# The shared expert's up products of one token block: sixteen 512-column matmuls replaced by seven products of two by two blocks

## The chip, the cores and the metric

The kernel runs on one core of one Trainium2 chip. The metric is the device time of one execution in microseconds (us); lower is better. The profile counts from the first to the last instruction (the span); a little time lies around the span and is part of the device time.

Engines, as the profile names them: PE (TensorE, matmuls) with PEld (its weight loads), DVE (VectorE), ACT (ScalarE), POOL (GpSimd, which here issues the gathers and scatters), SP (SyncE, which issues the plain DMAs).

## The reference

The input has 16 sequences of 128 tokens with 512 features, 2048 tokens in all. First comes cross attention with a residual, which the change does not touch. Then a mixture of experts:

```python
g = einsum('td,eid->tei', x, w1); u = einsum('td,eid->tei', x, w3)
a = silu(g) * u
routed = einsum('tei,edi,te->td', a, w2, comb)        # 32 experts, 8 for each token
sh = silu(x @ shared_w1.T) * (x @ shared_w3.T) @ shared_w2.T
out = routed + sh                                     # and the residual
```

Here `x` is the layer-normed input of 512 features, an expert's inner width is 256, and everything is float32. The change is in `sh`: the two "up" products `x @ shared_w1.T` and `x @ shared_w3.T` for the last 512 of the 2048 tokens.

## The kernel before

**Layout.** The normed tokens lie transposed in one buffer, `xall`, as four blocks `xnT[k]` of 512 tokens (128 partitions x 4 feature chunks x 512 tokens). `sup` holds the shared up weights (both matrices), `sdn` the shared down weight. `acts[k]` receives silu(g)*u of block `k`.

**Shared expert.** `shared_up(k, i, ...)` does one half (`i`) of the inner width of block `k`: four accumulating matmuls of 128x512 into one PSUM bank for `g`, four for `u`, a Silu on ACT (tile `ssl`) and a product on DVE (tile `sa`). `shared_down(b)` does two matmuls of 128x512 for the 128 tokens of sequence `b`, and `add_down` adds the result to the residual `xs[b]` on DVE and starts the DMA that writes it to the output. A product or an addition is not issued at once: it is put into the list `products` and issued some step later.

**Order.** The four compute engines run in an order written out by hand: each engine executes its instructions in the order in which the Python code issues them. The shared expert's matmuls fill PE while other engines work. Six of the eight halves (blocks 0 to 2) are done during the attention's end and the routing (`route`, then the loop over `slot_tokens`). After `finish_tokens` the list of each slot's token is known and POOL starts to gather rows. At this point the two halves of block 3 and eight down products are left. They are issued as follows:

```python
up_matmuls(2 * ND)                       # g and u of block 3, half 0: 8 matmuls
for f in evictions() + evictions(): f()
transpose_to(5)                          # the first five gathered slices
up_matmuls(2 * ND)                       # half 1: 8 matmuls
for f in evictions() + evictions(): f()
...
for i, b in enumerate(downs):            # b = 8..15
    shared_down(b, ps_p)
    ...                                  # transposes, block copies, weight sums, additions
```

**Gathered rows.** `gather(j)` (POOL) fetches the 128 rows of slice `j` into one of six buffers `xgs`; `transpose(j)` turns it on DVE in blocks of 32 (`blocks`) and `weigh(j)` takes its weights (tile `own`), after which the buffer is free for slice `j+6`. `block_copies(k)` copies the turned blocks of expert `k` (k in the order of execution) to `x_of[k % 3]`, which overlays `xall`: for experts 0 and 1 three quarters of these copies are on ACT and one quarter on DVE.

**Experts.** Expert 0 is computed directly (`up`, eight groups of four matmuls 128x256). Experts 1 to 30 use seven products of two by two blocks instead of eight (Strassen's scheme in Winograd's form): `weight_sums(k)` and `token_sums(k)` make four sums each on DVE, `product` issues the matmuls, and `seven(k)` is a generator that does one of the seven products at each `next` and schedules, with `soon`, the ACT copy of the first product (`p1`), the DVE additions (`u2`, `z`) and the Silu and multiplication one or more steps later. The fifth, sixth and seventh product accumulate into the banks of the first, third and fourth, so they need the earlier reader of that bank to be done. The bank pool `ps_p` has six banks, taken in turn; the last eight shared down products use it too.

Of the kernel before, what the change touches and what calls it, by code (L numbers as in the profile page):

```python
# [9 lines left out]
F32 = mybir.dt.float32  # L10
# [3 lines left out]
ALU = mybir.AluOpType  # L14
# [4 lines left out]
P = 128  # L19
# [8 lines left out]
NW = 3  # L28


ROOM = [704, 660, 640, 628, 616, 608, 604, 600, 596, 584, 580, 560, 544, 540, 540, 536]
# [6 lines left out]
ORDER = [18, 0, 11, 1, 29, 2, 3, 4]  # L38
# [8 lines left out]
def tile_xattn_moe(  # L47
# [15 lines left out]
    nc = tc.nc  # L63
    B, S, D = x.shape
    E, _, ND, I = w1.shape
    NI = I // P
    KV = D // HD // G
    NT = B
    NTB = NT // 4
    TB = 512  # L70
# [17 lines left out]
    xnT = [  # L88
        xall[:, k * ND * TB : (k + 1) * ND * TB].rearrange("p (d t) -> p d t", d=ND)
        for k in range(NTB)  # L90
    ]
# [58 lines left out]
    fp = x_only.enter_context(tc.tile_pool(name="fp", bufs=2, side="right"))  # L150
# [10 lines left out]
    sup = const.tile([P, 2, ND, I], F32, name="sup")  # L161
# [82 lines left out]
    def gate_logits(b, ps_lg):  # L244
# [15 lines left out]
    NA = 3  # L260
    aall = sap.tile([P, NA * NI * 2 * HM], F32, name="sa")
    acts = [
        aall[:, k * NI * TB : (k + 1) * NI * TB].rearrange("p (i t) -> p i t", i=NI)
        for k in range(NTB)
    ]
    acts_of = [
        aall[:, r * NI * 2 * HM : (r + 1) * NI * 2 * HM].rearrange("p (i t) -> p i t", i=NI)
        for r in range(NA)
    ]
# [733 lines left out]
    def experts(ups, in_order, later, products):  # L1003
# [8 lines left out]
        wup = [wp.tile([P, 2, ND, I], F32, name=f"wup{r}") for r in range(NW)]  # L1012
# [32 lines left out]
        shared = ExitStack()  # L1045
# [28 lines left out]
        def all_ups():  # L1074
            for k, i in ups:
                banks = iter(
                    [(ps_y, "y"), (ps_z, "y")]
                    if (k, i) == (1, 1)
                    else [(ps_p, "p")] * 2
                    if k == NTB - 1  # L1080
                    else [(ps_gu, "gu")] * 2
                )

                def bank():
                    pool, tag = next(banks)
                    return pool.tile([P, TB], F32, tag=tag, name="gu")

                yield from shared_up(k, i, bank, later, products)
# [3 lines left out]
        def up_matmuls(n):  # L1092
            for _ in range(n):
                next(matmuls, None)
# [259 lines left out]
        downs = iter(range(B))  # L1354
        held = []

        def evictions():
            nonlocal held
            fs = later + held
            held = list(products)  # L1360
            later.clear()
            products.clear()
            return fs
# [18 lines left out]
        pieces = []  # L1382
# [82 lines left out]
        def soon(f, after=1):  # L1465
            jobs.setdefault(now + after, []).append(f)
# [27 lines left out]
        M = TB // 2  # L1494
        sums = {}

        def weight_sums(k):


            a11, a12, a21, a22 = (  # L1500
                wup[k % NW][:, :, d : d + 2, ts(i, P)] for i in range(2) for d in (0, 2)
            )
            s1, s2, s4 = (
                tp.tile([P, 2, 2, P], F32, tag=name, name=name) for name in ("s1", "s2", "s4")
            )
            sums[k] = s1, s2, a21, s4
            return [
                lambda o=o, a=a, b=b, op=op: nc.vector.tensor_tensor(o, a, b, op)
                for o, a, b, op in (
                    (s1, a21, a22, ALU.add),  # L1510
                    (s2, s1, a11, ALU.subtract),
                    (a21, a11, a21, ALU.subtract),
                    (s4, a12, s2, ALU.subtract),
                )
            ]

        def halves_of(k):

            h = ROOM[ORDER[k]] // 2
            return [  # L1520
                x_of[k % NX][:, d : d + 2, i * h : (i + 1) * h] for d in (0, 2) for i in range(2)
            ]
# [29 lines left out]
                        skip_group_check=not first,  # L1552
                    )

        def add(out_, a, b):
            soon(lambda: nc.vector.tensor_tensor(out_, a, b, ALU.add))  # L1556

        def seven(k):


            h = ROOM[ORDER[k]] // 2
            act = acts_of[k % NA]
            a11, a12, _, a22 = (
                wup[k % NW][:, :, d : d + 2, ts(i, P)] for i in range(2) for d in (0, 2)
            )
            s1, s2, s3, s4 = sums[k]
            b11, _, b21, b22 = halves_of(k)
            t1, t2, t3, t4 = tsums.pop(k)
            both = 2 * h <= TB
            size = M if both else HM  # L1570

            def new(name, n, size, bufs=2):
                if name == "sg":
                    t = xnp.tile([P, TB], F32, tag="xn2", name=name, bufs=4)
                else:
                    size_of = 4 * M if name == "z" else TB
                    t = late.tile([P, size_of], F32, tag=name, name=name, bufs=bufs)
                return t[:, 0 : n * size].rearrange("p (n t) -> p n t", n=n)[:, :, 0:h]

            def silu(to, of, after):  # L1580
                soon(lambda: nc.scalar.activation(to, of, AF.Silu), after)

            def times(to, a, b, after):
                soon(lambda: nc.vector.tensor_tensor(to, a, b, ALU.mult), after)

            act0, act1 = act[:, 0, 0:h], act[:, 1, 0:h]
            act2 = act[:, :, h : 2 * h]

            for w in (slice(0, 2),) if both else (slice(0, 1), slice(1, 2)):

                many = w.stop - w.start

                def bank():
                    p = ps_p.tile([P, TB], F32, tag="p", name="p")
                    return p[:, 0 : many * size].rearrange("p (n t) -> p n t", n=many)[:, :, 0:h]

                pa, p1 = bank(), new("p1", many, size, 1)
                product(pa, a11[:, w], b11)
                soon(lambda p1=p1, pa=pa: nc.scalar.copy(p1, pa))
                yield  # L1600
                pb, u2 = bank(), new("u2", many, size)
                product(pb, s2[:, w], t2)
                add(u2, p1, pb)
                yield
                pc = bank()
                z = new("z", 2 * many, size)
                z0, z1 = z[:, 0:many], z[:, many : 2 * many]
                product(pc, s1[:, w], t1)
                add(z1, u2, pc)
                yield  # L1610
                pd = bank()
                product(pd, s3[:, w], t3)
                add(z1, z1, pd)
                yield
                product(pa, a12[:, w], b21, first=False)
                if both:
                    sl = new("sg", 1, TB)[:, 0]
                    silu(sl, pa[:, 0], 1)
                    times(act0, sl, pa[:, 1], 2)
                elif w.start == 0:  # L1620
                    silu(act0, pa[:, 0], 1)
                else:
                    times(act0, act0, pa[:, 0], 1)
                yield
                product(pc, s4[:, w], b22, first=False)
                add(z0, u2, pc)
                if both:
                    sl = new("sg", 2, M)
                    silu(sl, z[:, 0::2], 2)
                    times(act2, sl, z[:, 1::2], 3)  # L1630
                elif w.start == 0:
                    silu(act2, z, 2)
                else:
                    times(act2, act2, z, 2)
                yield
                product(pd, a22[:, w], t4, first=False)
                add(u2, u2, pd)
                if both:
                    sl = new("sg", 1, TB)[:, 0]
                    silu(sl, u2[:, 0], 2)  # L1640
                    times(act1, sl, u2[:, 1], 3)
                elif w.start == 0:
                    silu(act1, u2[:, 0], 2)
                else:
                    times(act1, act1, u2[:, 0], 2)
                yield
# [250 lines left out]
        def transpose_to(j):  # L1897
            nonlocal n_turned
            while n_turned < j:
                transpose(n_turned)  # L1900
                n_turned += 1
                gather_next()

        gather_next()
        up_matmuls(2 * ND)
        for f in evictions() + evictions():
            f()
        transpose_to(5)
        up_matmuls(2 * ND)
        for f in evictions() + evictions():  # L1910
            f()
        copies = [*block_copies(0), *block_copies(1, slices=range(4, 7))]
        copies = [f for _, _, f in copies]
        downs = list(downs)
        for i, b in enumerate(downs):
            shared_down(b, ps_p)
            transpose_to(min(6 + i, last_slice(3)))
# [114 lines left out]
        in_order.close()  # L2032
        ctx.close()

    pieces = [(k, i) for k in range(NTB) for i in range(NI)]
    left_over = attention_small()
    experts(pieces[1:], in_order, *left_over)
    left = nc.values_load(
# [64 lines left out]
```

## Time and profile before

| | us |
|---|---|
| median of 4 runs (849.90 to 851.83) | 850.63 |
| profiled execution, device time | 849.99 |
| its span | 848.1 |
| outside the span | 1.9 |
| PE busy | 830.0 (98%) |
| DVE busy | 686.4 (81%) |
| ACT busy | 670.8 (79%) |
| POOL busy | 479.0 (56%) |

The granted TensorE clock is 0.997 of full speed over the span. Where the code issues one float32 matmul, the profile shows two MATMUL rows, so 16 matmuls of block 3 are 32 rows. A row of the timeline gives start, duration, engine and line, operation, the written and the read tiles, shapes and a count; in square brackets stands how long the engine was idle before and what ended that.

### The profile page before, as it was taken

How to read it: one execution, taken by the hardware profiler on the slowest of the kernel's cores; microseconds unless marked ns; L12 is line 12 of the kernel's file. 1: busy time of each engine (PE TensorE's matmuls, PEld its weight loads, DVE VectorE, ACT ScalarE, POOL GpSimd, SP SyncE). 2: the span in 40 equal slices, each digit the busy share in tenths (PEclk: the TensorE clock that was granted, in tenths of full speed). 3: DMA queues.
4: the chain of work that ended last, by engine and by line, in shares of the span. 5: the costliest groups of instructions: out<-in, count | busy, mean ns of one | idle time of the engine just before them, and what ended most of it. 6: DMA issues, size and time to landing. Idle time of an engine off the chain costs nothing.

```text
span 848.1 us, 14951 instructions
## 1 busy us (share of the span) xinstructions
PE 830.0 (98%) x4847; PEld 604.1 (71%) x4847; DVE 686.4 (81%) x1660; ACT 670.8 (79%) x1225; POOL 479.0 (56%) x574
## 2 busy tenths in 40 slices
PE   8999999999999999999999999999999999999995
PEld 6555545546676866777787878787888899887663
DVE  7987888849787977988898989898989999986210
ACT  5989723638988896988988989988898999998631
POOL 4597730053445676465538585765757666654553
PEclk9999999999999999999999999999999999999998
DMA  9211104456666798577769697978788878785653
GB/s 298 81 52 64 58 33 159 152 157 199 177 153 152 172 190 240 135 187 177 190 156 228 166 218 179 219 170 197 180 201 191 209 193 184 195 209 123 97 83 50
DMA packets 59878, 137.22 MB, mean 162 GB/s; under 512 B 12168, under 2 KB 16392, under 8 KB 59792
## 3 DMA queue, kind: packets, MB, share of 16 engines
q0 software_dynamic: 32032, 69.25, 41.9%
q1 hardware_dynamic: 27680, 66.81, 23.5%
q8 instruction: 40, 0.66, 0.3%
q14 instruction: 46, 0.38, 0.1%
q10 hardware_dynamic: 80, 0.13, 0.1%
HBM read 96.71 MB, written 46.73 MB: 169 GB/s over the span
## 4 chain that ended last, share of the span: by engine, by line
PE 85%; DVE 5%; POOL 3%; issue 3%; ACT 2%; DMA 2%; POOLq 0%; ACTq 0%
PE p L1546 43%; PE y L1787 17%; PE gu L285 7%; PE y L1687 5%; PE y L1340 3%; PE m L491 2%; POOL out_dram L1659 2%; PE sc L473 2%; DMA out_dram<-yp,token 2%; PE gu L1476 2%; DVE o L501 1%; PE m L453 1%; ACT xall L1441 1%; DVE st L95 1%; PE tok L989 1%
## 5 line engine op out<-in xcount | busy, mean ns | idle before, releaser
L1441 ACT COPY xall<-blocks 32x512 f32<-32x512 f32 (+4 forms) x684 | 360.4, 527 | 10.9 <-DVE blocks L1444 0.9
L1659 POOL DMA_INDIRECT out_dram<-yp,token x122 | 201.0, 1648 | 153.0 <-ACT yp L1799 42.4
L1403 POOL DMA_INDIRECT xgs<-rows,token x138 | 152.9, 1108 | 120.2 <-DMA out_dram<-x 54.0
L1546 PE MATMUL p<-xall,wup 128*128 128x270 f32 (+27 forms) x720 | 185.9, 393 | 0.0
L1546 PEld LDWEIGHTS p<-xall,wup 128*128 128x128 f32 x720 | 136.7, 190 | 31.6 <-issue 4.7
L1546 PE MATMUL p<-t,s 128*128 128x270 f32 (+27 forms) x480 | 123.6, 394 | 0.0
L1546 PEld LDWEIGHTS p<-t,s 128*128 128x128 f32 x480 | 91.1, 190 | 20.2 <-issue 3.2
L1444 DVE STREAM_TRANSPOSE blocks<-xgs 128x512 f32<-128x512 f32 x138 | 97.0, 703 | 0.0
L1687 PE MATMUL y<-wdn,sa 128*32 128x512 f32 (+2 forms) x288 | 78.7, 596 | 0.0
L1659 POOL DMA_INDIRECT out_dram<-yw,token x28 | 45.0, 1605 | 49.5 <-DMA out_dram<-yw,token 29.8
L483 ACT ACTIVATE p<-sc 128x1024 f32<-128x1024 f32 x64 | 62.1, 1024 | 10.0 <-PE sc L473 9.3
L1556 DVE TENSOR_TENSOR z<-u,p 128x270 f32<-128x270 f32 (+27 forms) x96 | 48.4, 504 | 21.5 <-PE p L1546 21.2
L1546 PE MATMUL p<-t,wup 128*128 128x270 f32 (+27 forms) x240 | 63.8, 396 | 0.0
L1546 PE MATMUL p<-xall,s 128*128 128x270 f32 (+27 forms) x240 | 63.4, 395 | 0.0
L285 PE MATMUL gu<-xall,sup 128*128 128x512 f32 x128 | 58.7, 599 | 0.0
L1799 ACT ACTIVATE yp<-yp,wt 128x256 f32<-128x256 f32 (+1 forms) x96 | 54.3, 608 | 3.6 <-DVE yp L1778 2.6
L1778 DVE TENSOR_TENSOR yp<-sdn,y 128x512 f32<-128x512 f32 x72 | 49.1, 682 | 8.2 <-PE y L1787 4.6
L1546 PEld LDWEIGHTS p<-t,wup 128*128 128x128 f32 x240 | 45.0, 190 | 14.7 <-DVE z L1556 2.8
L1546 PEld LDWEIGHTS p<-xall,s 128*128 128x128 f32 x240 | 45.3, 190 | 13.0 <-issue 3.9
L1787 PE MATMUL y<-sup,sa 128*128 128x256 f32 x192 | 49.9, 382 | 1.5 <-ACT sdn L1842 1.4
L1687 PEld LDWEIGHTS y<-wdn,sa 128*32 128x32 f32 (+2 forms) x288 | 28.0, 145 | 30.1 <-issue 28.2
L1787 PE MATMUL y<-wdn,sa 128*128 128x256 f32 x192 | 49.3, 379 | 0.0
(235 smaller groups left out, 1392.8 us busy)
## 6 DMA issues: line engine op xcount, KB each, us to landing
wup<-in_w_dram SPq DMA_DIRECT2D x64, 512.0 KB, 6.6
wdn<-in_w_dram SPq DMA_DIRECT2D x32, 512.0 KB, 4.8
rows<-xn SPq DMA_DIRECT2D x16, 256.0 KB, 2.2
out_dram<-x SPq DMA_DIRECT2D x16, 256.0 KB, 3.0
x<-in_x_dram SPq DMA_DIRECT2D x15, 256.0 KB, 6.0
xgs<-rows,token POOLq DMA_INDIRECT x138, 5.4
out_dram<-yp,token POOLq DMA_INDIRECT x122, 5.6
cTs<-in_cT_dram SPq DMA_DIRECT2D x4, 256.0 KB, 5.2
```

Of the source, the lines that this page charges most:

```text
L285: nc.tensor.matmul(acc, lhsT=sup[:, w, d, ts(i, P)], rhs=xnT[k][:, d, :], start=(d == 0), stop=(d == ND - 1),)
L483: nc.scalar.activation(p, sc, AF.Exp, scale=1.0 / HD**0.5)
L1403: nc.gpsimd.indirect_dma_start(out=t, out_offset=None, in_=rows[:, :], in_offset=bass.IndirectOffsetOnAxis(ap=token[:, j : j + 1], axis=0) ...
L1441: yield on_ACT, 1 + many, lambda dst=dst, of=of, copy=copy: copy(dst, of)
L1444: nc.vector.transpose(blocks[:, j % NB_BUF, :], xgs[:, j % NG_BUF, 0:D])
L1546: nc.tensor.matmul(acc[:, i, 0:h], lhsT=w[:, i, d, :], rhs=x[:, d, :], start=(first and i == d == 0), stop=(i == outs[-1] and d == 1), ski ...
L1556: soon(lambda: nc.vector.tensor_tensor(out_, a, b, ALU.add))
L1659: ins = nc.gpsimd.indirect_dma_start(out=flat, out_offset=bass.IndirectOffsetOnAxis(ap=token2[:, k - 1 : k] if a else token[0:b, j : j + 1 ...
L1687: nc.tensor.matmul(y[c0:c1, :], lhsT=acts_of[k % NA][:, i, col : col + c1 - c0], rhs=wdn[k % NW][:, i, :], start=(i == 0), stop=(i == NI - 1),
L1778: then(lambda: nc.vector.tensor_tensor(to, a, b, op), after)
L1787: nc.tensor.matmul(acc[:, r, :], lhsT=a[:, ts(r, P)], rhs=b, start=(first and r == 0), stop=(r == 1), skip_group_check=not first,)
L1799: lambda r=r, at=at: nc.scalar.activation(to[:, r], of[:, r], AF.Copy, scale=wt[:, at : at + 1]),
```

## The change

The two halves of block 3 are no longer done by `shared_up`. Instead `seven` gets a form for the shared expert: block 3 of the tokens is cut into two by two blocks (256 features x 256 tokens each), the up weight `sup` likewise, and seven products of four matmuls 128x256 replace sixteen matmuls of 128x512. The sums are made on DVE right before (`shared_sums`): S1, S2, S3, S4 of the weights (S3 in place in `sup`) and t1, t2, t3, t4 of the tokens (t3 in place in `xnT[3]`; t1, t2 and t4 in the unused `xnT[1]`). Temporaries (`p1`, `u2`, `z`) lie in the unused `xnT[2]`. Two down products, b = 8 and 9, stand behind the second and the fifth of the seven; six are left for the loop behind. The five transposes that stood together between the halves are spread behind the third to seventh product.

```diff
-        up_matmuls(2 * ND)
-        for f in evictions() + evictions():
+        later_jobs = {}
+        turn = 0
+        ...
+        k = NTB - 1
+        sums_of_k = shared_sums(k)
+        of_shared = seven(k, True, lambda f, after=1: later_jobs.setdefault(turn + after, []).append(f))
+        downs = list(downs)
+        for f in sums_of_k[:4]:
             f()
-        transpose_to(5)
-        up_matmuls(2 * ND)
-        for f in evictions() + evictions():
+        for down_too in (0, 1, 0, 0, 1, 0, 0, 0):
+            behind = list(products)
+            products.clear()
+            next(of_shared, None)
+            if down_too:
+                shared_down(downs.pop(0), ps_p)
+            for f in behind:
+                f()
+            run_later()
+            for f in sums_of_k[4:] if turn == 1 else ():
+                f()
+            transpose_to(max(0, min(turn - 2, 5)))
+        while later_jobs:
+            run_later()
+        for f in products:
             f()
+        products.clear()
         copies = [*block_copies(0), *block_copies(1, slices=range(4, 7))]
         copies = [f for _, _, f in copies]
-        downs = list(downs)
         for i, b in enumerate(downs):
             shared_down(b, ps_p)
```

```diff
+        def shared_sums(k):
+            b11, b12, b21, b22 = shared_halves(k)
+            t1, t2, t4 = (
+                xnT[1].rearrange("p d (a t) -> p (d a) t", t=M)[:, 2 * i : 2 * i + 2]
+                for i in range(3)
+            )
+            tsums[E + k] = t1, t2, b12, t4
+            s1, s2, s3, s4 = weight_sums(E + k, sup)
+            t1, t2, t3, t4 = (
+                lambda o=o, a=a, b=b: nc.vector.tensor_tensor(o, a, b, ALU.subtract)
+                for o, a, b in ((t1, b12, b11), (t2, b22, t1), (b12, b22, b12), (t4, b21, t2))
+            )
+            return [s1, s2, t1, t2, t3, s3, s4, t4]
...
+        def seven(k, shared=False, soon=soon):
...
-    pieces = [(k, i) for k in range(NTB) for i in range(NI)]
+    pieces = [(k, i) for k in range(NTB - 1) for i in range(NI)]
```

As built, the order on each engine from the end of the routing to expert 0 is (matmuls as the code counts them, transposes T with their weighing):

| | before | after |
|---|---|---|
| PE | 16 of 128x512, downs 8 to 15 | P1 (4 of 128x256), P2, down 8, P3, P4, P5, down 9, P6, P7, downs 10 to 15 |
| DVE | add of down 7, product, T0 to T4, product, T5 | add of down 7, S1, S2, t1, t2, t3, S3, S4, t4, u2, add of down 8, z, T0, z, T1, T2, add of down 9, product, z, T3, u2, T4, two products, T5 |
| ACT | Silu, Silu, then the copies of expert 0 | copy of p1, three Silus, then the copies of expert 0 |

In the loop over the downs the copies are dealt over six turns instead of eight. The orders of POOL and SP are unchanged, and so is everything from expert 0 on.

More of the change, by code (lines that the diff above doesn't have):

```diff
@@ L1078, in all_ups @@
                     if (k, i) == (1, 1)
-                    else [(ps_p, "p")] * 2
-                    if k == NTB - 1
                     else [(ps_gu, "gu")] * 2
@@ L1495, in experts, with weight_sums @@
         sums = {}
-        def weight_sums(k):
+        def weight_sums(k, of=None):
+            of = wup[k % NW] if of is None else of
             a11, a12, a21, a22 = (
-                wup[k % NW][:, :, d : d + 2, ts(i, P)] for i in range(2) for d in (0, 2)
+                of[:, :, d : d + 2, ts(i, P)] for i in range(2) for d in (0, 2)
             )
@@ L1553, in product, with shared_halves, add @@
                     )
[L1555 to L1562, printed above, removed]
+        def shared_halves(k):
+            return [xnT[k][:, d : d + 2, i * M : (i + 1) * M] for d in (0, 2) for i in range(2)]
+        def shared_sums(k):
[12 more added lines that the diff above has]
+        def seven(k, shared=False, soon=soon):
+            h = M if shared else ROOM[ORDER[k]] // 2
+            act = acts[k] if shared else acts_of[k % NA]
             a11, a12, _, a22 = (
-                wup[k % NW][:, :, d : d + 2, ts(i, P)] for i in range(2) for d in (0, 2)
-            )
-            s1, s2, s3, s4 = sums[k]
-            b11, _, b21, b22 = halves_of(k)
-            t1, t2, t3, t4 = tsums.pop(k)
+                (sup if shared else wup[k % NW])[:, :, d : d + 2, ts(i, P)]
+                for i in range(2)
+                for d in (0, 2)
+            )
+            s1, s2, s3, s4 = sums[E + k if shared else k]
+            b11, _, b21, b22 = shared_halves(k) if shared else halves_of(k)
+            t1, t2, t3, t4 = tsums.pop(E + k if shared else k)
             both = 2 * h <= TB
             size = M if both else HM
+            def add(out_, a, b):
+                soon(lambda: nc.vector.tensor_tensor(out_, a, b, ALU.add))
             def new(name, n, size, bufs=2):
+                if shared:
+                    if name == "sg":
+                        t = fp.tile([P, TB], F32, tag="ssl", name="ssl")
+                        return t.rearrange("p (n t) -> p n t", n=n)[:, :, 0:h]
+                    at = dict(p1=0, u2=2, z=4)[name]
+                    return xnT[2].rearrange("p d (a t) -> p (d a) t", t=M)[:, at : at + n]
                 if name == "sg":
@@ L1904, in experts, with run_later @@
         gather_next()
-        up_matmuls(2 * ND)
-        for f in evictions() + evictions():
-            f()
-        transpose_to(5)
-        up_matmuls(2 * ND)
-        for f in evictions() + evictions():
+        later_jobs = {}
+        turn = 0
+        def run_later():
+            nonlocal turn
+            turn += 1
+            for f in later_jobs.pop(turn, []):
+                f()
[4 more added lines that the diff above has]
+        for f in sums_of_k[:4]:
+            f()
+        for down_too in (0, 1, 0, 0, 1, 0, 0, 0):
[8 more added lines that the diff above has]
+            for f in sums_of_k[4:] if turn == 1 else ():
+                f()
+            transpose_to(max(0, min(turn - 2, 5)))
+        while later_jobs:
+            run_later()
+        for f in products:
             f()
+        products.clear()
         copies = [*block_copies(0), *block_copies(1, slices=range(4, 7))]
         copies = [f for _, _, f in copies]
-        downs = list(downs)
         for i, b in enumerate(downs):
```

## The prediction

> **What bounds the kernel now.** I read the page first, then the chain of waits around the change, then the timelines of PE, DVE, ACT and POOL from 172 to 240 us.
>
> ```profile
> PE 830.0 (98%) x4847; PEld 604.1 (71%) x4847; DVE 686.4 (81%) x1660; ACT 670.8 (79%) x1225; POOL 479.0 (56%) x574
> ```
>
> PE is busy nearly throughout. The chain of waits (start, duration, what, rows) passes through nothing but PE at the change:
>
> ```profile
> 172.68 1.76 PE y L1340 x4
> 174.44 13.73 PE gu L285 x32
> 188.18 13.73 PE y L1340 x32
> 201.91 13.81 PE gu L1476 x64
> 215.72 4.73 PE p L1546 x16
> 220.46 1.72 PE y L1687 x4
> 222.18 8.28 PE p L1546 x28
> ```
>
> So here PE's own time, and any new wait of PE, goes one to one into the end. (The chain books a matmul 0.16 us later than the timeline starts it; below I use the timeline.) Now the two engines that feed PE, DVE first:
>
> ```profile
> 174.48 0.69 DVE L1350 TENSOR_TENSOR x<-y,x 128x512 f32<-128x512 f32 x1 [0.53 <-PE y L1340]
> 181.42 0.69 DVE L296 TENSOR_TENSOR sa<-ssl,gu 128x512 f32<-128x512 f32 x1 [6.25 <-PE gu L285]
> ...
> 189.99 0.67 DVE L1508 TENSOR_TENSOR s<-wup 128x512 f32<-128x512 f32 x1
> 190.70 0.69 DVE L1508 TENSOR_TENSOR s<-s,wup 128x512 f32<-128x512 f32 x1
> 191.31 0.68 DVE L1508 TENSOR_TENSOR wup<-wup 128x512 f32<-128x512 f32 x1
> 191.91 0.68 DVE L1508 TENSOR_TENSOR s<-wup,s 128x512 f32<-128x512 f32 x1
> ...
> 206.40 0.71 DVE L1444 STREAM_TRANSPOSE blocks<-xgs 128x512 f32<-128x512 f32 x1
> ...
> 218.20 0.52 DVE L1556 TENSOR_TENSOR u<-p,p 128x352 f32<-128x352 f32 x1 [0.33 <-PE p L1546]
> ```
>
> DVE waits 6.25 us for PE while block 3's first half runs; from 188.3 to 218 it has no gap. The L1508 rows are the sums of an expert, of the size the new ones have: a sum starts 0.61 us after the one before, 0.71 us if it reads its result. ACT:
>
> ```profile
> 185.41 7.53 ACT L1441 COPY xall<-blocks 32x512 f32<-32x512 f32 x12
> 193.85 7.80 ACT L1441 COPY xall<-blocks 32x384 f32<-32x384 f32 x15 [0.92 <-DVE blocks L1444]
> 203.68 0.39 ACT L1485 ACTIVATE sg<-gu 128x256 f32<-128x256 f32 x1 [2.03 <-PE gu L1476]
> ```
>
> Expert 0's copies end at 192.9, 8.8 us before PE starts expert 0 at 201.75. That slack is what the change will use.
>
> **Part 1, PE work.** Removed: 32 rows of 128x512, 13.73/32 = 0.429 us each. Added: 7 x 4 x 2 = 56 rows of 128x256; the nearest row, L1476, has 64 of this shape in 13.81, 0.216 each, so 12.08 (1.73 a product). Saved: 1.65 us. The eight downs cost the same (1.72 each).
> A rule speaks against this. The Trainium skill, "TensorE: Matmul & The Clock Gate", section "Back-to-back issue gap", says that in a stream of weight loads and matmuls the spacing is set by both, about 81 ns at 128 columns and 131 ns at 512. Interpolated to 256 columns (my estimate, 98 ns), 56 rows would cost 1.3 times what 32 wide ones do, and the seven products would lose. The float32 rows here contradict it: 0.216 against 0.429 is proportional to the columns, with the 0.19 us weight load hidden under either.
>
> **Part 2, the wait of the second product.** P1 needs no sum; P2 needs S2 and t2. DVE runs in order, behind the add of down 7, which cannot start before 174.48 as PE finishes that down only then: S1 174.48 + 0.61 = 175.09, S2 + 0.71 = 175.80 (its start), t1 + 0.61 = 176.41, t2 + 0.71 = 177.12, done 177.80, handed over by 177.86. P1 runs 174.28 to 176.01. PE waits 1.85 us, with downs 8 to 15 queued behind P2 on PE. Bounds: 1.7 (the chain's later booking of PE) and 2.0 (a handover of 0.2, as from PE to DVE above). So parts 1 and 2 sum to **+0.2**: the saving is gone at once.
>
> **Part 3, the rest of the seven, hidden.** t3, S3, S4, t4 (177.7 to 180.2) and u2 (180.2) run beside P2 and down 8 (to 181.3). P3 181.3, P4 183.0, P5 184.8, down 9 to 188.2, P6 188.2, P7 189.9 to 191.65. The copy of p1 has ended long before P5; z, 183.2 to 183.9, before P6. Behind P7: u2 191.85 to 192.5, Silu 192.6 to 193.0, last product 193.85 to 194.25. Down 12 is the first to need it, at 195.1; downs 10 and 11 cover it with 0.8 to spare, and without them it would cost 2.6. PE reaches expert 0 at 201.95.
> POOL is moved past nothing, but gathers 1 to 5 now run beside sums. Bounds from rows: 1.00 us for most, 1.54 for the one at 190.00 that began with an L1508 sum. Five times 0.54 makes gather 5 land 2.7 later, still before its transpose at 194.2: nothing. The Trainium skill, "SBUF — State Buffer", section "Who interferes with whom", says that a tensor_tensor with two SBUF inputs blocks GpSimd's reads for the whole instruction; the 1.54 row fits a delay of most of one sum.
>
> **Part 4, the backlog.** In before, T3 ends at 185.0 and T5 at 189.8. After, T3 stands behind z of P6 (190.1) and runs 190.7 to 191.5, T5 194.2 to 195.0. DVE is 5.2 us late, less two adds already made (1.2) and small gaps: the row at 206.40 comes at about 210.0, 3.6 late. ACT starts expert 0's copies at 193.0 behind the last Silu, 7.6 late; it makes up its gaps of 0.92 and 2.03, so the row at 203.68 comes at about 208.3, 4.6 late. Three places where PE meets this:
> - Expert 0 needs 12 copies on ACT (193.0 + 7.53 = 200.5: in time) and four on DVE: T5's end 195.0, four sums and four turns of add, transpose and copy as before (8.3 us from 189.66 to 197.9 in before, one add and one transpose less now) give 202.1. PE waits 0 to 0.5; I take 0.2.
> - Expert 1, first half. PE needs z from DVE for P6 and P7. In before (start of the z adds 219.31 and 221.12, 0.52 each; PE at 223.19 and 224.38) the slack is 3.3 and 2.7 us. DVE arrives at u2 (218.20 in before) 3.6 to 4.5 late (the 0.33 gap is made up, and u2 also waits for ACT's copy of p1, 4.1 to 4.8 late); PE itself is 0.4 late. The wait is between 0.4 and 1.8; I take 1.1.
> - Expert 1, second half. Expert 2's token sums stand before u2 on DVE and wait for ACT's copies, still 3.5 late; slack at P7 there is 2.1, PE then 1.6 late. 0 to 0.8; I take 0.4.
>
> Behind this the gaps of DVE (1.8, 0.5) and ACT (0.8, 0.8, 1.3) between 236 and 245 take up the rest.
>
> **Sum.** +0.2 + 0.2 + 1.1 + 0.4 = +1.9: the profiled execution goes from 849.99 to 851.9 (span 848.1 + 1.9 and 1.9 around it). The median of the runs lies 0.6 above that execution, so I predict 850.63 + 1.9 = **852.5**.
>
> **Rivals.**
> - *Backlog absorbed* (no change): DVE and ACT arrive only as late as their slack. For it: each margin is within 1 us of the lateness. Against it: DVE has no gap from 188 to 218. Parts 1 and 2 and half of the copies' wait remain, +0.2 to +0.6: 850.8 to 851.2.
> - *Sums in time* (faster): S2 and t2 are ready at P1's end. It decides from t2 done by 176.0, and then -1.65: 849.0; each 0.1 later takes 0.1 back. Against it: 3.3 us of chain behind an add that PE itself releases at 174.48. It would need the scheduler to let PE's next down go first, and the order as built has P2 first.
> - *Backlog lasts* (slower still): ACT, 4 us late, does not recover before 245, since its load from 215 to 230 is 14.0 of 15 us. Then the copies for experts 2 and 3 hold DVE's sums, and PE waits 0.5 to 1 us in each of two to four further halves: +3.5 to +5.5, 854.1 to 856.1.
> - That the change does not do what it says is excluded: the built order shows the seven products and two downs between.
>
> **How the numbers follow.** Forecast 0.50 (+1.2 to +2.8), absorbed 0.22, lasting 0.18, faster 0.10. The range takes the first two and most of the third: 850.4 (0.6 under the absorbed case's middle) to 855.0. 0.2% is 1.7 us, about what a measurement of this kernel tells from no change. Of the forecast's band 0.30 lies above it, 0.20 below; so slower 0.30 + 0.18 = 0.48, same 0.20 + 0.22 = 0.42, faster 0.10.
>
> **What would show it.** Right: a PE gap of 1.7 to 2.0 us before the second product, released by DVE; PE at expert 0 within 0.5 of 201.95; ACT's copies of expert 0 from about 193; PE gaps before the sixth and seventh product of expert 1, released by DVE z. Wrong: P2 starting near 176.0, or no PE wait from 202 to 240, or waits going on behind 245.

## The result and the profile after

The changed kernel is a little slower: 852.0 us (median of 31 runs, 851.75 to 853.33) against 850.21 us (median of 51 runs of the kernel before, taken with it, 849.80 to 852.12); the ratio is 1.0019, 95% interval 1.0014 to 1.0024. The profiled execution took 851.85 us, its span is 850.0 (848.1 before). The span grew by the 1.9 us that were forecast.

PE of the changed kernel at the change, from its timeline (start, duration, engine, line, shapes, rows, and in brackets the idle time before and who ended it):

```profile
174.17 1.89 PE L1545 MATMUL p<-xall,sup 128*128 128x256 f32 x8
177.77 1.99 PE L1545 MATMUL p<-xall,s 128*128 128x256 f32 x8 [1.71 <-DVE xall L1568]
...
181.31 1.89 PE L1545 MATMUL p<-xall,s 128*128 128x256 f32 x8
183.04 3.62 PE L1545 MATMUL p<-xall,sup 128*128 128x256 f32 x16
...
191.66 10.46 PE L1338 MATMUL y<-sdn,sa 128*128 128x512 f32 x24
202.15 14.05 PE L1474 MATMUL gu<-xall,wup 128*128 128x256 f32 x64
216.04 1.35 PE L1545 MATMUL p<-xall,wup 128*128 128x352 f32 x4
...
225.72 1.45 PE L1545 MATMUL p<-t,wup 128*128 128x352 f32 x4 [0.35 <-DVE z L1590]
...
236.19 1.45 PE L1545 MATMUL p<-t,wup 128*128 128x352 f32 x4 [0.20 <-DVE z L1590]
237.48 1.11 PE L1545 MATMUL p<-xall,wup 128*128 128x280 f32 x4
```

The first two rows are P1 and P2. Eight rows of 128x256 take 1.73 from start to start (181.31 to 183.04 for P3), so P1 ends at 175.9 and PE stands for 1.87 before P2; the row books 1.71 of it, because P1's row lasts 1.89, longer than the 1.73 from start to start. P2 itself takes 1.83 to the start of down 8 (179.60), 0.10 more than a product that did not have to wait. Expert 0 starts at 202.15, right behind the last two of DVE's four copies of it (201.20 to 202.06). In expert 1 (from 216.04) the seventh product waits for DVE's z in both halves, and in the first half the sixth comes late too.

The times from start to start, without the 0.1 us by which this execution reached the change earlier:

| stretch on PE | before | after | difference |
|---|---|---|---|
| first matmul of block 3 to expert 0 | 27.47 | 27.98 | +0.51 |
| expert 0 | 13.81 | 13.89 | +0.08 |
| expert 1, first half | 10.00 | 10.97 | +0.97 |
| expert 1, second half | 10.00 | 10.47 | +0.47 |

The sum is +2.03, and less the 0.11 of the earlier start, expert 2 begins 1.92 later than before (237.48 against 235.56). From there to the end nothing is lost or won.

DVE of the changed kernel, from its timeline:

```profile
174.37 0.69 DVE L1348 TENSOR_TENSOR x<-y,x 128x512 f32<-128x512 f32 x1 [0.53 <-PE y L1338]
174.98 0.68 DVE L1507 TENSOR_TENSOR s<-sup 128x512 f32<-128x512 f32 x1
175.69 0.69 DVE L1507 TENSOR_TENSOR s<-s,sup 128x512 f32<-128x512 f32 x1
176.30 2.01 DVE L1568 TENSOR_TENSOR xall<-xall 128x512 f32<-128x512 f32 x3
...
210.19 0.71 DVE L1442 STREAM_TRANSPOSE blocks<-xgs 128x512 f32<-128x512 f32 x1
...
222.32 0.52 DVE L1590 TENSOR_TENSOR u<-p,p 128x352 f32<-128x352 f32 x1 [0.66 <-ACT p L1625]
...
229.65 0.74 DVE L1536 TENSOR_TENSOR t<-xall 128x560 f32<-128x560 f32 x1 [1.27 <-ACT xall L1439]
...
232.69 0.52 DVE L1590 TENSOR_TENSOR u<-p,p 128x352 f32<-128x352 f32 x1 [1.52 <-ACT p L1625]
```

The add of down 7, S1, S2, then t1, t2 and t3 in one merged row: this is the chain that P2 waits for. The transpose that stood at 206.40 stands at 210.19. At 222.32, 229.65 and 232.69 DVE itself waits, for ACT. ACT's timeline:

```profile
193.09 15.36 ACT L1439 COPY xall<-blocks 32x512 f32<-32x512 f32 x27
...
221.84 0.45 ACT L1625 COPY p<-p 128x352 f32<-128x352 f32 x1
```

Behind the last of block 3's Silus (192.65) the copies start at 193.09 instead of 185.41, run without a gap to the first Silu of expert 0 (208.47 instead of 203.68), and the copy of p1 of expert 1 comes at 221.84 instead of 217.42.

### The profile page after: what moved, and what is told of

It reads as the page before. It is cut to its first block, busy times and chain, and to the rows that moved or that the text cites. A ratio compares the mean times of both kernels' runs of the same rounds, so it can differ in the third digit from the quotient of the medians.

```text
span 850.0 us, 15018 instructions
## 1 busy us (share of the span) xinstructions
PE 829.0 (98%) x4871; PEld 607.6 (71%) x4871; DVE 693.9 (82%) x1674; ACT 671.4 (79%) x1227; POOL 476.0 (56%) x574
## 4 chain that ended last, share of the span: by engine, by line
PE 76%; DVE 6%; ACT 5%; issue 4%; DMA 4%; POOL 4%; POOLq 0%; ACTq 0%
PE p L1545 41%; PE y L1813 17%; PE gu L285 5%; ACT xall L1439 4%; DMA out_dram<-yp,token 4%; PE y L1713 4%; POOL out_dram L1685 3%; PE m L491 2%; PE sc L473 2%; PE y L1338 2%; DVE o L501 1%; PE m L453 1%; DVE st L95 1%; PE tok L989 1%; DVE xq L136 1%
## 5 line engine op out<-in xcount | busy, mean ns | idle before, releaser
L1685 POOL DMA_INDIRECT out_dram<-yp,token x122 | 199.0, 1631 | 157.5 <-ACT yp L1825 49.5
L1545 PE MATMUL p<-xall,s 128*128 128x256 f32 (+27 forms) x264 | 69.3, 394 | 1.8 <-DVE xall L1568 1.7
L1545 PEld LDWEIGHTS p<-xall,s 128*128 128x128 f32 x264 | 49.7, 190 | 16.9 <-issue 4.9
L1813 PE MATMUL y<-sup 128*128 128x256 f32 x192 | 49.3, 379 | 0.0
```

What stands on the lines that cost most here:

```text
L1545: nc.tensor.matmul(acc[:, i, 0:h], lhsT=w[:, i, d, :], rhs=x[:, d, :], start=(first and i == d == 0), stop=(i == outs[-1] and d == 1), ski ...
L1685: ins = nc.gpsimd.indirect_dma_start(out=flat, out_offset=bass.IndirectOffsetOnAxis(ap=token2[:, k - 1 : k] if a else token[0:b, j : j + 1 ...
L1813: nc.tensor.matmul(acc[:, r, :], lhsT=a[:, ts(r, P)], rhs=b, start=(first and r == 0), stop=(r == 1), skip_group_check=not first,)
```

## The experiments

Each kernel was measured in five rounds beside the kernel before on the same chip (e1 to e4 on one chip, e5 to e7 on another). "To expert 0" is from the first matmul of block 3 to the first of expert 0, "expert 1" the length of its two halves, both on PE. The values of before and after are repeated for comparison.

| kernel | ratio to before, 95% interval | span | to expert 0 | expert 1 |
|---|---|---|---|---|
| before | | 848.1 | 27.47 | 20.00 |
| after | 1.0019 [1.0014, 1.0024] | 850.0 | 27.98 | 21.44 |
| e1 down 8 behind P1 | 1.0004 [0.9995, 1.0013] | 848.4 | 26.26 | 21.45 |
| e2 early transposes and copies | 1.0002 [0.9993, 1.0011] | 848.5 | 27.80 | 20.00 |
| e3 both | 0.9981 [0.9972, 0.9990] | 846.6 | 26.08 | 20.03 |
| e4 before, late transposes | 1.0015 [1.0006, 1.0024] | 849.9 | 27.97 | 20.01 |
| e5 early transposes only | 1.0015 [1.0006, 1.0024] | 849.9 | 27.79 | 21.71 |
| e6 sums first | 1.0002 [0.9993, 1.0010] | 849.0 | 26.77 | 21.43 |
| e7 all three edits | 0.9974 [0.9965, 0.9984] | 846.6 | 25.82 | 20.00 |

### e1: down 8 behind the first product

```diff
-        for down_too in (0, 1, 0, 0, 1, 0, 0, 0):
+        for down_too in (1, 0, 0, 0, 1, 0, 0, 0):
```

> Order of PE: P1, down 8, P2 instead of P1, P2, down 8; nothing else. Theory (order): the 1.71 us that PE waits before P2 is covered by down 8's 1.72, P2 starts near 177.7 with under 0.2 of wait, expert 0 starts near 200.4 instead of 202.15, and since DVE and ACT are early by as much as PE, the waits of expert 1 (1.4 us in all) stay: span 848.2 to 848.5, level with before (848.1) and 1.5 to 1.8 under the changed kernel (850.0). Rival (the wait moves): P3 or P4 waits instead, because DVE is full with sums until 180.2: span 849.5 to 850.0. Rival (products dearer than their rows): expert 0 starts no earlier than 201.5.

PE's timeline of this kernel:

```profile
176.02 1.88 PE L1338 MATMUL y<-sdn,sa 128*128 128x512 f32 x4
177.89 3.72 PE L1545 MATMUL p<-xall,s 128*128 128x256 f32 x16
...
200.55 14.05 PE L1474 MATMUL gu<-xall,wup 128*128 128x256 f32 x64
...
224.13 1.45 PE L1545 MATMUL p<-t,wup 128*128 128x352 f32 x4 [0.35 <-DVE z L1590]
```

Down 8 (176.02) fills the place in which PE stood. It takes 1.72, so 0.15 of wait is left before 177.89, and P3 follows P2 without one (they share a row). Expert 0 comes 1.72 earlier after P1 than in the changed kernel; expert 1 stays as long (21.45 against 21.44). The rivals (the wait moves to P3, or the products cost more than their rows) are out.

### e2: transposes and copies into the gaps

```diff
-            transpose_to(max(0, min(turn - 2, 5)))
+            transpose_to((0, 0, 1, 3, 4, 5, 5, 5, 5)[turn])
+            for _ in range((0, 0, 0, 0, 0, 4, 4, 2, 0)[turn]):
+                copies.pop(0)()
```

(`copies` is made ahead of the loop.)

> The changed kernel with transposes T0 to T4 one or two products earlier and ten of expert 0's sixteen copies between the fifth and the seventh product, in gaps of DVE and ACT. Theory (order makes the backlog): the wait before P2 stays at 1.7, but DVE reaches its eleventh transpose near 208 instead of 210.2 and ACT its first Silu of expert 0 near 204.5 instead of 208.5; the PE waits before expert 0 (0.2) and in expert 1 (1.4) go: span 848.3 to 848.7. Rival (amount): the 8 us of DVE work that the change adds makes the backlog whatever the order, the waits of expert 1 stay: span 849.6 to 850.2.

PE's waits in this kernel from 172 to 300 us (who waited for whom, us in total, times, longest) are one line, where the changed kernel has waits for z as well:

```profile
PE p L1545 <- DVE xall L1568: 1.7, 1, 1.7
```

ACT's timeline:

```profile
187.23 3.75 ACT L1439 COPY xall<-blocks 32x512 f32<-32x512 f32 x6
...
220.19 0.45 ACT L1625 COPY p<-p 128x352 f32<-128x352 f32 x1
```

All of the change's DVE work is still there, and expert 1 takes 20.00 as in before. So the order makes the backlog harmful here, not the amount of work. Two sizes were missed: DVE's eleventh transpose comes at 209.12 (208 was expected), and ACT's first Silu of expert 0 at 206.82 (204.5 was expected), the second because ACT now waits 3.13 us for the transpose of slice 6. It is enough: 1.65 us earlier at the copy of p1 and the waits are gone.

### e3: both edits

> Both edits of the two kernels before at once. Theory (order): the saving of 1.65 us on PE is left over, less at most 0.3 of small waits: expert 0 starts near 200.3, no PE wait from 202 to 240 but under 0.3, span 846.5 to 847.0, which is 1.1 to 1.6 under before. Rival (amount): the waits of expert 1 stay, span 848.0 to 848.5. Rival (products dearer): no better than before, 848.1 or more.

As the theory had it: to expert 0 26.08, expert 1 20.03, span 846.6. This is the first version that beats both kernels, by 0.19% of before.

### e4: the kernel before with late transposes

```diff
-        transpose_to(5)
         up_matmuls(2 * ND)
         for f in evictions() + evictions():
             f()
+        transpose_to(5)
```

> The kernel before, without the seven products; only the five transposes T0 to T4 are moved from between the two halves of block 3 to behind them. PE's work and DVE's work are those of before. Theory (order makes the backlog): T3 ends near 191.9 as in the changed kernel (191.4), expert 0's copies on ACT start near 192 instead of 185.4, DVE is 3.9 late, and PE waits in expert 1 like in the changed kernel: span 849.1 to 849.8, 1.0 to 1.7 over before. Rival (amount of DVE work, or the seven products themselves): no PE wait, 848.1.

Slower than before without any of the seven products, as the theory said, but PE waits elsewhere. The timelines of PE, of its weight loads (PEld) and of DVE:

```profile
202.03 14.44 PE L1476 MATMUL gu<-xall,wup 128*128 128x256 f32 x64 [0.33 <-issue]
```

```profile
207.56 8.50 PEld L1476 LDWEIGHTS gu<-xall,wup 128*128 128x128 f32 x40 [0.52 <-ACT sg L1485]
```

```profile
201.50 0.42 DVE L1441 COPY xall<-blocks 32x512 f32<-32x512 f32 x1
...
210.05 0.71 DVE L1444 STREAM_TRANSPOSE blocks<-xgs 128x512 f32<-128x512 f32 x1
```

PE reaches expert 0 0.5 late, right behind the last of DVE's four copies of it (201.50 + 0.42), and expert 0 itself takes 14.27 instead of 13.81: a weight load waits 0.52 us for ACT's first Silu. Expert 1 takes 20.01. DVE is as late as in the changed kernel (210.05 against 210.19), yet PE does not wait for it there; ACT's copies had started 1.3 us earlier (191.75), and u2 runs at 221.44 without a wait for ACT. The expectation named the wrong place. The ratio puts the loss at 1.3 us and the medians at 0.9 (850.81 against 849.90), where 1.0 to 1.7 was expected. In the profiled execution 0.8 us more were lost on a single wait for z between 500 and 600 us, which is why its span lies farther over before (1.8) than the ratio says.

### e5: early transposes alone

```diff
-            transpose_to(max(0, min(turn - 2, 5)))
+            transpose_to((0, 0, 1, 3, 4, 5, 5, 5, 5)[turn])
```

> The changed kernel with only the transposes T0 to T5 earlier (as in the kernel with early turns); the copies of expert 0 stay behind the last Silu on ACT. It tells which engine's lateness makes PE wait in expert 1. Theory (ACT decides: in the changed kernel DVE's u2 waits 0.66 us for ACT's copy of p1): DVE reaches its eleventh transpose about 1.4 earlier, near 208.8, but ACT's first Silu of expert 0 stays at 208.4 and its p1 copy at 221.8, so u2 and z come as before and the PE waits stay: span 849.6 to 850.0. Rival (DVE's lateness decides): the waits shrink by most of 1.4, span 848.4 to 848.9.

This was asked because of e4: which engine's lateness counts? The timeline of DVE, and of PE:

```profile
209.34 0.71 DVE L1442 STREAM_TRANSPOSE blocks<-xgs 128x512 f32<-128x512 f32 x1
...
222.21 0.52 DVE L1590 TENSOR_TENSOR u<-p,p 128x352 f32<-128x352 f32 x1 [1.25 <-ACT p L1625]
```

```profile
225.61 1.45 PE L1545 MATMUL p<-t,wup 128*128 128x352 f32 x4 [0.35 <-DVE z L1590]
```

DVE is earlier at its eleventh transpose (by 0.85, not the 1.4 expected) and then only waits longer for ACT, 1.25 instead of 0.66; u2 stays where it was (222.21 against 222.32) and so does the seventh product (225.61 against 225.72). PE reaches expert 0 without the wait of 0.19 and loses that time again in expert 1 (21.71 instead of 21.44). The time that DVE gained bought nothing: of the two late engines, ACT is the later one and decides. A kernel that relieves ACT alone was not run. DVE had only 0.66 us to spare at u2, so about 0.3 of the first half's 0.97 would have stayed without the earlier transposes; this is an estimate from these rows.

### e6: the four sums ahead of the add

The sums S1, S2, t1, t2 are issued ahead of the add of down 7, which PE releases only at 174.37. (`add_of_seven` holds that add; the code further up no longer issues it.)

```diff
-        for f in sums_of_k[:4]:
+        for f in sums_of_k[:4] + add_of_seven:
             f()
```

> The changed kernel with S1, S2, t1, t2 ahead of the add of down 7 on DVE instead of behind it. Theory (P2 waits for a chain of four sums that the add holds back): the chain starts at 173.7 instead of 174.98, t2 is done 1.2 earlier, the wait before P2 falls from 1.71 to 0.5, expert 0 starts near 200.95, the waits of expert 1 stay: span 848.7 to 849.0. Rival (PE waits for something else there, a PSUM bank or the add itself): the wait stays, 850.0.

PE's timeline:

```profile
176.58 1.99 PE L1546 MATMUL p<-xall,s 128*128 128x256 f32 x8 [0.49 <-DVE xall L1569]
```

The wait falls from 1.71 to 0.49, and expert 0 comes at 200.97. So the wait before P2 was the chain of four sums and the add in front of it, nothing of PSUM. The span is 849.0; the ratio's interval includes 1.

### e7: all three edits

> Down 8 ahead of P2, early transposes and copies, and the four sums ahead of the add of down 7. Theory: PE has no wait left between 174 and 240, expert 0 starts 25.8 to 25.9 after P1 (7 x 1.73 + 8 x 1.72 = 25.85), 0.15 to 0.2 better than without the third edit: span 846.3 to 846.6. Rival (the third edit only moves work of DVE): level with the kernel of both edits, 846.6 or a little more.

PE's timeline:

```profile
177.63 3.62 PE L1546 MATMUL p<-xall,s 128*128 128x256 f32 x16
...
200.01 13.98 PE L1475 MATMUL gu<-xall,wup 128*128 128x256 f32 x64
```

P2 starts at once behind down 8. To expert 0 it takes 25.82, which is 1.65 less than before: exactly what the rows priced the seven products at (7 x 1.726 + 8 x 1.717 = 25.82). Against e3 this stretch is 0.26 shorter, where 0.15 to 0.2 was expected. The 0.3 us by which expert 2 starts earlier than in e3 does not show in the span (846.6 in both), and the intervals of the two ratios overlap; whether the third edit is worth anything behind this stretch is open.

## Why the prediction was right, point by point

- **PE's saving** (forecast 1.65): right, and shown by itself in e7. The spacing of the rows is proportional to the columns: P3 and P4 start 1.73 apart, 0.216 a row at 256 columns, against 0.429 at 512. The rule of the Trainium skill ("TensorE: Matmul & The Clock Gate", section "Back-to-back issue gap"), from which the products would have lost, does not hold for these float32 rows.
- **P2's wait** (forecast 1.85): 1.87 from start to start. e6 and e1 show its cause: take the add away from in front, or put 1.72 us of PE work into it, and it shrinks from 1.87 to 0.65 and 0.15 (all from start to start). Not foreseen: the 0.10 that P2 itself takes longer behind the wait. With it the stretch to expert 0 adds up: -1.65 + 1.87 + 0.10 + 0.19 = +0.51, where +0.4 was forecast.
- **The rest of the seven hidden**: right. P3 to P7 follow without a gap, down 12 does not wait.
- **Gathers beside sums**: POOL's rows in the changed kernel are

```profile
175.17 1.36 POOL L1401 DMA_INDIRECT xgs<-rows,token  x1 [0.30 <-issue]
176.83 1.03 POOL L1401 DMA_INDIRECT xgs<-rows,token  x1 [0.30 <-issue]
178.16 1.02 POOL L1401 DMA_INDIRECT xgs<-rows,token  x1 [0.30 <-issue]
179.49 1.50 POOL L1401 DMA_INDIRECT xgs<-rows,token  x1 [0.30 <-issue]
```

  Two of four were stretched, by 0.36 and 0.50 over the usual 1.00, less than the bound of 0.54 each, and no transpose waited. The lock that the Trainium skill describes ("SBUF — State Buffer", section "Who interferes with whom") does not fit all four: the middle two, wholly beside sums, show almost nothing (1.03 and 1.02). The same section infers that generating the descriptors of a DMA needs the write interface, which such a sum leaves free; by that the other two would not have been stretched either. What stretched them is open.
- **The wait before expert 0** (forecast 0.2, for DVE's copies): 0.19, what is left between 191.66 + 24 x 0.429 = 201.96 and 202.15; DVE's last copy ends at 202.06, where 202.1 was forecast. Not foreseen: 0.08 inside expert 0.
- **Expert 1** (forecast 1.1 and 0.4): 0.97 and 0.47. The sizes were right, the readings behind them only in part. I worked the first wait out from DVE's lateness and the slack of its z adds, and named ACT's copy of p1 only as a second condition. e5 shows that ACT's lateness (4.4 us at that copy) decides; DVE had 0.66 us to spare. The two happened to be nearly equal here, which is why the first term came out: that is luck. The second term is luck too. Its own figures (3.5 late, a slack of 2.1, PE 1.6 late) leave no wait, and 0.4 was the middle of a range whose upper end was not worked out. The token sums did wait for ACT's copies as described (229.65 against 226.20, 3.45 late), but behind them u2 waited 1.52 more for ACT's copy of p1 and came 3.85 late (232.69 against 228.84), and that set the z before the seventh product.
- **The backlog ends by 245**: right. From expert 2 on, the changed kernel's PE has the three waits for `sdn` (1.4 us in all) that before has too, and no other.
- **The median**: 852.0 against the 852.5 forecast; the difference of 1.8 was forecast as 1.9, and the kernel before had a median 0.4 lower in the 51 runs than in the four that I had.

Of the rivals, "absorbed" fails by the waits in expert 1, "sums in time" by the 1.87, "lasting" by the clean stretch behind 238. The size lies at the border that I drew at 0.2%: +0.19%, with an interval (0.14% to 0.24%) that excludes no change and has the border inside, so the result does not decide between the forecast's "slower" and "same".

## What to carry to other kernels

Fewer multiplications on the bound engine are worth only what the order lets through: here 1.65 us of saved PE time were paid back by four sums that PE had to wait for (1.87) and by a queue of copies that a late Silu held up (1.4). When an algorithm needs operands that another engine makes at the last moment, put work that needs none of them between (down 8 was at hand), and look at what stands behind the new waits in each in-order queue. When two engines are late, relieve each alone before concluding which one the bound engine waits for: the releaser named at PE was DVE's z, but DVE was waiting for ACT. Here only DVE was relieved alone, and then both.

## What the hardware showed that was not expected

Some gathers are stretched beside DVE sums and some are not (1.36 and 1.50 against 1.03 and 1.02), with no pattern that these four rows settle. A product before which PE had stood took 0.10 to 0.11 us longer from start to start: P2 1.83 instead of 1.73, the seventh products of expert 1 1.29 instead of 1.18; why is open. The standing of 1.87 us did not change the granted clock, which is 1.00 both from 174 to 178 and from 178 to 190.
